# Fewer instructions for the edge lists, and earlier weights, in a four-layer graph network on one core

## The chip, the cores and the metric

The kernel runs on one core of one Trainium2 chip. A core has TensorE (PE, matrix products; PEld are its weight loads), VectorE (DVE), ScalarE (ACT), GpSimd (POOL) and SyncE (SP), each with its own queue of instructions that runs in order, and 16 DMA engines that they share. The metric is the device time of one execution, in microseconds, as the median of several runs.

## The reference

A graph of 3327 nodes with 512 features each and an integer adjacency matrix (a few edges per row, more in the first rows and columns). Four layers run on it, each as `x = layernorm(x + layer(x))`.

```python
# layer 0 and layer 3: attention over the neighbours (layer 3 builds its weights from four quaternion parts)
Wh = einsum('nd,hdo->hno', x, W)                       # 8 heads of 64
e  = leaky_relu(f1[:, :, None] + f2[:, None, :], 0.2)  # f1 = Wh.a1, f2 = Wh.a2
out = elu(softmax(where(adj > 0, e, -9e15)) @ Wh)
# layer 1: mean over the neighbours
agg = (adj > 0) @ x / max(deg, 1)
out = relu(concat(x @ W_self + b_self, agg @ W_nb + b_nb) @ W_comb + b_comb)
# layer 2: mean over the first 64 neighbours of each row, leaky relu, plus leaky relu of x @ W_line.T
```

## The kernel before

The nodes stand in 26 blocks of 128. The adjacency is sparse, so the kernel doesn't multiply with it: for each block it makes a list of its edges, and in each layer an indirect DMA (on POOL's queue, line 999) gathers the rows of the neighbours, 128 edges to a "chunk", into a ring of slots in SBUF. A product with a 0/1 selection matrix sums the gathered rows into the block's nodes (L1356 in layers 0 and 3, L1850 in layers 1 and 2). Rows are gathered in groups of up to four chunks (`GROUP`). Block 0, whose rows are dense, is done apart.

**The prologue** has three interleaved parts. `projection(b)` loads a block of x, transposes it (L783) and multiplies it with layer 0's weights (L1037), and stores the result in the table `t0_d`. `structure` reads the adjacency rows of one block after the other (L866), takes their signs on ScalarE with a running sum (L873), and makes the block's list. `fused_weights` multiplies layer 1's self and neighbour weights by its combining weights, eight tiles of 512x128, each transposed (L783 on `raw`) and multiplied (L800), and a bias product at its end (L1634). `score_weights` (L1551 to L1554) prepares layer 0's scores from the weights `w0` and the vectors `a0`. The loop over t starts a projection, then takes three steps of `structure`, and from t = 13 on one step of `fused_weights`; whatever is left of the fused weights is drained after the last projection and after `g0.head` and `g0.finish`, which complete the table.

**A list** is made so: VectorE multiplies the mask with a code of positions (L888), finds the largest eight of each of several segments (L901) and of those the largest K (L911, L913). Its degree and the entry for the first column (`dgs`, L889, L896, L897) are rounded to `dg16` (L921). TensorE turns the degrees of 128 rows into starting places with two products (L923, L924) in the PSUM tile p1; four ScalarE and three VectorE instructions (L926 to L932) take from it the biases `here`, the places `starts` and `nmids`, and the first two columns of `sl`. A further product (L935) gives the steps `dl`. Then for each span of up to ten chunks, first those that fill the room from its near end, then those of its far end, ScalarE makes a sign matrix `u` (L945), TensorE multiplies it (L952), ScalarE rounds the result (L955), and VectorE picks the edge (L960 to L973). p1, p2 and a transposed column share one PSUM bank.

The first 16 or so lists are made in the prologue, the rest during layer 0, whose `feed` takes one or two steps of `structure` for each group. Until layer 1 begins, a scheduler orders the instructions of each engine by priorities and estimates; from there (`manual_schedule`) they stand in the order of the program. The memory of the ring (22 slots of 528 floats) is lent during the prologue, in order of the calls of `lent`, to the mask of block 0, `w0`, `a0`, the rows of zeros, a scratch row, and the combining weights `wc`; a gather into a slot waits for the readers of what lay there.

`groups` takes sizes for its first groups from its argument `first`; in the kernel before only layer 3 passes `(1, 2)`.

Of the kernel before, what the change touches and what calls it, by code (L numbers as in the profile page):

```python
# [631 lines left out]
def sparse_path(ctx, tc, flag_i, x, adj, l0_w, l0_a1, l0_a2, l1_w_self, l1_b_self, l1_w_nb, l1_b_nb,  # L632
# [68 lines left out]
    starts = keep.tile([P, NL, 2], F32, name="starts")  # L701
    nmids = keep.tile([P, NL, 2], F32, name="nmids")
    for l in (l for ls in lists for l in ls):
        l.nmid = nmids[:, l.at]
# [47 lines left out]
    point5 = const.tile([P, 1], F32, name="point5")  # L752
    nc.gpsimd.memset(point5, 0.5)
# [98 lines left out]
    def structure(big, mid, ps, m0):  # L852
# [16 lines left out]
        def masks(b, ab):  # L869
            ms = []  # L870
            for s in range(2):
                m = m0[:, s * HW:(s + 1) * HW] if b == 0 else big.tile([P, HW], BF16, name="m", bufs=2)
                nc.scalar.activation(m, ab[s], AF.Sign, accum_out=half[:, s, b:b + 1])  # L873
                ms.append(m)
            return ms
# [3 lines left out]
        for k, b in enumerate(order):  # L879
# [9 lines left out]
            nc.vector.tensor_reduce(dgs[:, b - 1, 1:2], ms[0][:, :P], AX.X, ALU.add)  # L889
# [3 lines left out]
            for l in lists[b]:  # L893
                L, K, cuts, a = l.L, l.K, l.cuts, l.at
                dg = dgs[:, a, 0:1]
                nc.vector.tensor_scalar(dg, half[:, 0, b:b + 1], half[:, 1, b:b + 1], 1.0, ALU.add, ALU.max)  # L896
                nc.vector.tensor_sub(dg, dg, dgs[:, a, 1:2])  # L897
# [9 lines left out]
                sl = mid.tile([P, K + 2], F32, name="sl")  # L907
                slots = sl[:, 2:]
# [11 lines left out]
                dg16 = mid.tile([P, 2], BF16, name="dg16")  # L920
                nc.vector.tensor_copy(dg16, dgs[:, a])  # L921
                p1 = ps.tile([P, 512], F32, name="p1", tag="lp")
                nc.tensor.matmul(p1[:, 0:2], before, dg16, start=True, stop=True)  # L923
                nc.tensor.matmul(p1[:, 2:4], middle, dg16, start=True, stop=True)  # L924
                here = mid.tile([P, 2], F32, name="here")
                nc.scalar.activation(here[:, 0:1], p1[:, 0:1], AF.Identity, bias=point5, scale=-1.0)  # L926
                nc.vector.tensor_scalar(here[:, 1:2], p1[:, 1:2], -1.0, l.room - 0.5, ALU.mult, ALU.add)
                nc.scalar.copy(starts[:, a], p1[:, 0:2])
                nc.scalar.copy(sl[:, 0:1], p1[:, 0:1])
                nc.vector.scalar_tensor_tensor(sl[:, 1:2], p1[:, 1:2], 1.0 - l.room, dg, ALU.add, ALU.subtract)  # L930
                nc.scalar.activation(l.nmid[:, 0:1], p1[:, 2:3], AF.Identity, bias=ones[:, 0:1])
                nc.vector.tensor_scalar(l.nmid[:, 1:2], p1[:, 3:4], -1.0, 1.0 - 2 * l.room, ALU.mult, ALU.add)  # L932
                yield None
                p2 = ps.tile([P, 512], F32, name="p2", tag="lp")
                nc.tensor.matmul(p2[:, :K + 2], step, sl, start=True, stop=True)  # L935
# [5 lines left out]
                spans = [(0, c0, l.up) for c0 in range(0, l.up, G)] + [(1, c0, L) for c0 in range(l.down, L, G)]  # L941
                for far, c0, end in spans:
                    g = min(G, end - c0)
                    u = mid.tile([P, g * P], BF16, name="u")
                    nc.scalar.activation(u, place[:, c0 * P:(c0 + g) * P], AF.Sign, bias=here[:, far:far + 1],  # L945
                                         scale=-1.0 if far else 1.0)
                    if not far:
                        yield None
                    pv = ps.tile([P, 512], F32, name="pv")
                    for c in range(g):  # L950
# [4 lines left out]
                    nc.scalar.copy(vc[:, :g * W], pv[:, :g * W])  # L955
                    if not far:
                        yield None
                    v = vc[:, :g * W].rearrange("p (c k) -> p c k", k=W)
                    off = mid.tile([P, g, 1], I16, name="off")
                    nc.vector.tensor_sub(off[:, :, 0], (npos if far else pos)[:, c0:c0 + g], v[:, :, 1 + far])  # L960
                    eq = mid.tile([P, g, K], I16, name="eq")
                    nc.vector.tensor_tensor(eq, slot[:, None, :K].to_broadcast([P, g, K]),
                                            off.to_broadcast([P, g, K]), ALU.is_equal)
                    nc.vector.tensor_mul(eq, eq, v[:, :, 3:])
                    hit = mid.tile([P, g], I16, name="hit")
                    with nc.allow_low_precision(reason="whole numbers below 4096"):
                        nc.vector.tensor_reduce(hit, eq, AX.X, ALU.add)
                    at = l.idx[:, c0:c0 + g]
                    if far:
                        nc.vector.tensor_tensor(at, at, hit, ALU.add)  # L970
                        continue
                    nc.vector.scalar_tensor_tensor(at, hit, P + 1.0, hit, ALU.is_gt, ALU.mult)
                    nc.vector.scalar_tensor_tensor(l.dst[:, c0:c0 + g], hit, P + 1.0, v[:, :, 0],  # L973
                                                   ALU.is_gt, ALU.mult)
# [45 lines left out]
    class Gat:  # L1020
# [242 lines left out]
        def group(self, item, pools, accs, done, sall=None):  # L1263
# [22 lines left out]
            for t, k, q0, q1 in parts:  # L1286
                if q0 < q1:
                    o = t[:, q0 * P:q1 * P] if t is far else t[:, :(q1 - q0) * P]
                    nc.scalar.activation(o, place[:, (c0 + q0) * P:(c0 + q1) * P], AF.Abs,  # L1289
                                         bias=l.nmid[:, k:k + 1], scale=2.0)  # L1290
# [284 lines left out]
    code = iota("code", NP, U16, 1, 2, 0, big)  # L1575
    mid = pool_in(listlay, "l0mid")
# [3 lines left out]
    with ExitStack() as pro:  # L1580
# [10 lines left out]
        w0 = lent(DC * (D + 3 * H0)).rearrange("p (c s o) -> p c s o", c=DC, s=2)  # L1591
        for c in range(DC):
# [79 lines left out]
        for t in range(NB):  # L1672
# [3 lines left out]
            if t == 13:  # L1676
                fused.add(fused_weights())
# [509 lines left out]
```

## Time and profile before

| | |
|---|---|
| median of 3 runs | 1666.48 us (1666.45 to 1667.93) |
| profiled execution | 1770.79 us, of which the span 1769.0 |
| mean granted clock of TensorE in it | 0.928 of full |
| busy in the span | PE 86%, DVE 67%, ACT 52%, POOL 43% |
| last projection ends | 205.5 us |
| first gather of layer 0 starts | 214.5 us |
| last list's segments searched (L901) | 411 us |
| layer 0 to layer 1, first gather of layer 1 | 746 us |
| first gather of layer 2 | 1137 us |

The profiled execution is one execution with the profiler on; times of single instructions come from it. Busy times are the union of an engine's instructions; an engine's share says how full it is, not whether the end waits for it. A line number is that of the kernel before unless another is said.

### The profile page before, as it was taken

The page shows a single profiled execution, that of the slowest core. Times are in us where ns is not written, and L with a number is a line of the kernel's source. Part 1 is how long each engine was busy: PE and PEld are TensorE (multiplying, and loading weights), DVE is VectorE, ACT ScalarE, POOL GpSimd, SP SyncE. Part 2 cuts the span into 40 slices and gives each one's busy share as a digit, 9 for nine tenths or more (in the row PEclk, how much of TensorE's full clock was granted, in tenths as well). Part 3 has the DMA queues.
Part 4 walks back from the last instruction along what each step waited for, and adds up shares of the span by engine and source line. Part 5 has one row for each costly group of instructions (what it writes and reads, how often), then busy time and mean ns, then how long its engine had stood idle before and what let it go on. Part 6 is the DMA issues. An engine that isn't in the chain of part 4 may idle for free.

```text
span 1769.0 us, 24447 instructions
## 1 busy us (share of the span) xinstructions
PE 1514.6 (86%) x7266; PEld 1006.2 (57%) x7266; DVE 1187.4 (67%) x3292; ACT 911.9 (52%) x3026; POOL 753.8 (43%) x909
## 2 busy tenths in 40 slices
PE   5979848899999999889999999867799983978985
PEld 4756536656666777445555554423566763756764
DVE  8988948988567788125656785537566642857886
ACT  5879745666767778312122221201344442657897
POOL 3000146564454520164444652266666305666650
PEclk9989978999999999889999999988899996989898
DMA  8787667666665542198888995287878406677761
GB/s 257 240 279 239 212 194 239 222 198 189 190 183 159 163 132 79 66 406 296 300 292 303 336 366 201 98 284 246 268 251 267 167 37 193 183 206 211 225 204 56
DMA packets 130402, 381.99 MB, mean 216 GB/s; under 512 B 22037, under 2 KB 36477, under 8 KB 130259
## 3 DMA queue, kind: packets, MB, share of 16 engines
q0 software_dynamic: 67696, 252.97, 45.1%
q1 hardware_dynamic: 62563, 127.35, 21.4%
q8 instruction: 60, 0.98, 0.2%
q14 instruction: 83, 0.68, 0.1%
HBM read 331.89 MB, written 48.37 MB: 215 GB/s over the span
## 4 chain that ended last, share of the span: by engine, by line
PE 59%; DVE 14%; ACT 9%; issue 8%; DMA 4%; another core or an unknown queue 3%; POOL 2%; SPq 0%; ACTq 0%; POOLq 0%; DVEq 0%
PE po L800 18%; PE acc L1356 12%; PE acc L1850 9%; PE po L1037 9%; PE pt L783 3%; DVE cand L901 2%; DVE gt L1337 2%; PE acc L1244 1%; PE acc L1842 1%; DMA gm<-t_d,idx 1%; ACT h L1507 1%; DVE val L888 1%; ACT gd L1457 1%; PE acc L1929 1%
## 5 line engine op out<-in xcount | busy, mean ns | idle before, releaser
L999 POOL DMA_INDIRECT gt<-t_d,idx x201 | 201.6, 1003 | 380.0 <-DVE mx L1136 200.4
L999 POOL DMA_INDIRECT gl<-t_d,idx x265 | 263.8, 995 | 185.4 <-issue 59.4
L1356 PE MATMUL acc<-gt,sel 128*128 128x264 f32 (+3 forms) x804 | 210.7, 407 | 3.3 <-DVE gt L1337 1.3
L800 PE MATMUL po<-wn,xt 128*128 128x512 f32 x416 | 197.6, 618 | 16.8 <-ACT vc L955 5.3
L999 POOL DMA_INDIRECT gm<-t_d,idx x138 | 136.4, 988 | 133.0 <-PE acc L1850 79.5
L1356 PEld LDWEIGHTS acc<-gt,sel 128*128 128x128 f32 (+3 forms) x804 | 151.0, 197 | 41.1 <-issue 15.0
L1356 PE MATMUL acc<-gl,sel 128*128 128x260 f32 (+3 forms) x524 | 138.9, 407 | 12.1 <-issue 11.7
L800 PEld LDWEIGHTS po<-wn,xt 128*128 128x128 f32 x416 | 79.2, 197 | 103.4 <-issue 82.1
L1037 PE MATMUL po<-gt,xt 128*128 128x268 f32 x416 | 115.6, 423 | 15.4 <-ACT xt L790 11.2
L1337 DVE TENSOR_TENSOR gt<-gt,pg 128x1536 f32<-128x1536 f32 (+3 forms) x63 | 116.5, 1849 | 14.3 <-ACT sel L1332 12.8
L1356 PEld LDWEIGHTS acc<-gl,sel 128*128 128x128 f32 (+3 forms) x524 | 98.7, 198 | 31.3 <-issue 17.5
L1037 PE MATMUL po<-w,xt 128*128 128x262 f32 x416 | 101.8, 399 | 12.8 <-ACT xt L790 6.9
L1850 PE MATMUL acc<-gm,selr 128*128 128x512 f32 (+3 forms) x324 | 107.6, 455 | 5.4 <-DMA gm<-t_d,idx 5.0
L786 ACT COPY xt<-pt 128x512 f32<-128x512 f32 x81 | 47.0, 588 | 119.5 <-PE pt L783 93.7
L901 DVE MAX8 cand<-val 128x8 f32<-128x464 uint16 (+32 forms) x184 | 107.8, 619 | 0.0
L999 POOL DMA_INDIRECT gk<-t_d,idx x65 | 65.7, 1011 | 98.0 <-DMA t_d<-mean 60.3
L1037 PEld LDWEIGHTS po<-w,xt 128*128 128x128 f32 x416 | 81.0, 197 | 32.0 <-ACT xt L790 11.6
L1037 PEld LDWEIGHTS po<-gt,xt 128*128 128x128 f32 x416 | 78.4, 202 | 34.5 <-ACT xt L790 14.5
L800 PE MATMUL po<-wx,xt 128*128 128x512 f32 x208 | 93.6, 595 | 0.4 <-issue 0.3
L1289 ACT ACTIVATE far<-place,nmids 128x384 int16<-128x384 int16 (+3 forms) x167 | 87.3, 541 | 11.9 <-DVE ds L1299 9.4
L800 PE MATMUL po<-wl,xt 128*128 128x512 f32 x208 | 93.0, 592 | 0.0
L783 PE MATMUL pt<-s_ident,xres 128*128 128x128 f32 x500 | 79.1, 286 | 12.3 <-DVE xres L845 5.3
(389 smaller groups left out, 3283.0 us busy)
## 6 DMA issues: line engine op xcount, KB each, us to landing
ab<-in_adj_dram SPq DMA_DIRECT2D x25, 832.0 KB
ab<-in_adj_dram SPq DMA_DIRECT2D x25, 831.5 KB
t_d<-t SPq DMA_DIRECT2D x25, 512.0 KB
gm<-t_d POOLq DMA_DIRECT2D x23, 512.0 KB
t_d<-t SPq DMA_DIRECT2D x25, 384.0 KB
t_d<-tg SPq DMA_DIRECT2D x25, 264.0 KB
gd<-t_d SPq DMA_DIRECT2D x25, 264.0 KB
t_d<-tg SPq DMA_DIRECT2D x25, 260.0 KB
```

The costliest lines, as they stand in the source:

```text
L783: nc.tensor.transpose(pt[:, c, :], src[:, c * P:(c + 1) * P], ident)
L786: nc.scalar.copy(xt, pt)
L800: nc.tensor.matmul(po, xt[:, c, :], w[:, c], start=c == 0, stop=c == DC - 1)
L888: nc.vector.tensor_mul(val[:, s * HW:(s + 1) * HW], ms[s], code[:, s * HW:(s + 1) * HW])
L901: nc.vector.max(out=cand[:, s, :], in_=val[:, cuts[s]:cuts[s + 1]])
L999: nc.gpsimd.indirect_dma_start(out=t[:m, c, :], out_offset=None, in_=table[:, :], in_offset=bass.IndirectOffsetOnAxis(ap=l.idx[:m, c0 + c: ...
L1037: nc.tensor.matmul(pw[s], xt[:, c, :], self.w[:, c, s, :], start=c == 0, stop=c == DC - 1)
L1244: nc.tensor.matmul(self.acc[h // hh][:, h % hh, :], wt[:m, h, :], G[:m, h, :], start=False, stop=False)
L1289: nc.scalar.activation(o, place[:, (c0 + q0) * P:(c0 + q1) * P], AF.Abs, bias=l.nmid[:, k:k + 1], scale=2.0)
L1337: nc.vector.tensor_mul(Gc[:, :, :OUT], Gc[:, :, :OUT], w[:, :g].rearrange("p c (h o) -> p (c h) o", o=1).to_broadcast([P, g * H, OUT]))
L1356: nc.tensor.matmul(accs[b][s], S[:m, c, :], G[:m, c, s * hh * M:(s + 1) * hh * M], start=at + c == 0, stop=last)
L1850: nc.tensor.matmul(accs[b], chosen, parts[:, k * D:(k + 1) * D], start=at + c + k == 0, stop=k == top and at + c == n - 1)
```

## The change

Four edits. (1) The lists: the degree in the first 128 columns comes from a separate Sign with its own running sum on ScalarE, so VectorE's reduction goes; p1 is summed from five products with constants (`halves`, `rooms`) so that all eight columns come out ready, and two ScalarE copies take them; the far span joins the last near span where both fit in ten chunks. (2) The attention vectors are loaded before `w0`, and x three blocks ahead of its projection. (3) `fused_weights` starts at t = 9, and yields once more before its bias product; its `wc` is thereby lent before the rows of zeros. (4) The first two groups of layers 0, 1 and 2 have one and two chunks.

```diff
-    starts = keep.tile([P, NL, 2], F32, name="starts")
-    nmids = keep.tile([P, NL, 2], F32, name="nmids")
+    sites = keep.tile([P, NL, 4], F32, name="sites")
+    starts = sites[:, :, :2]
...
-    point5 = const.tile([P, 1], F32, name="point5")
-    nc.gpsimd.memset(point5, 0.5)
+    signs = const.tile([P, 3, 2], F32, name="signs")
+    nc.gpsimd.memset(signs, 1.0)
+    nc.gpsimd.memset(signs[:, 0], -1.0)
+    ones16 = const.tile([1, P], BF16, name="ones16")
+    nc.gpsimd.memset(ones16, 1.0)
+    halves = const.tile([1, 8], BF16, name="halves")
+    for k, v in enumerate((0.5, -0.5, 0.0, 1.0, 0.0, 0.0, 1.0, 1.0)):
+        nc.gpsimd.memset(halves[:, k:k + 1], v)
...
-                nc.scalar.activation(m, ab[s], AF.Sign, accum_out=half[:, s, b:b + 1])
+                c0 = P if b and s == 0 else 0
+                if c0:
+                    nc.scalar.activation(m[:, :P], ab[s][:, :P], AF.Sign, accum_out=dgs[:, b - 1, 1:2])
+                nc.scalar.activation(m[:, c0:], ab[s][:, c0:], AF.Sign, accum_out=half[:, s, b:b + 1])
...
-            nc.vector.tensor_reduce(dgs[:, b - 1, 1:2], ms[0][:, :P], AX.X, ALU.add)
...
-                nc.vector.tensor_scalar(dg, half[:, 0, b:b + 1], half[:, 1, b:b + 1], 1.0, ALU.add, ALU.max)
-                nc.vector.tensor_sub(dg, dg, dgs[:, a, 1:2])
+                nc.vector.tensor_add(dg, half[:, 0, b:b + 1], half[:, 1, b:b + 1])
+                nc.vector.scalar_tensor_tensor(dg, dgs[:, a, 1:2], 0.0, dg, ALU.is_equal, ALU.max)
...
-                dg16 = mid.tile([P, 2], BF16, name="dg16")
-                nc.vector.tensor_copy(dg16, dgs[:, a])
+                dg16 = mid.tile([P, 3, 2], BF16, name="dg16")
+                nc.vector.tensor_mul(dg16, signs, dgs[:, a, None, :].to_broadcast([P, 3, 2]))
                 p1 = ps.tile([P, 512], F32, name="p1", tag="lp")
-                nc.tensor.matmul(p1[:, 0:2], before, dg16, start=True, stop=True)
-                nc.tensor.matmul(p1[:, 2:4], middle, dg16, start=True, stop=True)
-                here = mid.tile([P, 2], F32, name="here")
-                nc.scalar.activation(here[:, 0:1], p1[:, 0:1], AF.Identity, bias=point5, scale=-1.0)
-                nc.vector.tensor_scalar(here[:, 1:2], p1[:, 1:2], -1.0, l.room - 0.5, ALU.mult, ALU.add)
-                nc.scalar.copy(starts[:, a], p1[:, 0:2])
-                nc.scalar.copy(sl[:, 0:1], p1[:, 0:1])
-                nc.vector.scalar_tensor_tensor(sl[:, 1:2], p1[:, 1:2], 1.0 - l.room, dg, ALU.add, ALU.subtract)
-                nc.scalar.activation(l.nmid[:, 0:1], p1[:, 2:3], AF.Identity, bias=ones[:, 0:1])
-                nc.vector.tensor_scalar(l.nmid[:, 1:2], p1[:, 3:4], -1.0, 1.0 - 2 * l.room, ALU.mult, ALU.add)
+                nc.tensor.matmul(p1[:, :8], ones16, halves, start=True, stop=False)
+                nc.tensor.matmul(p1[:, :8], ones16, rooms[:, a], start=False, stop=False)
+                d6 = dg16.rearrange("p k s -> p (k s)")
+                nc.tensor.matmul(p1[:, :6], before, d6, start=False, stop=False)
+                nc.tensor.matmul(p1[:, 3:4], ident16, d6[:, 0:1], start=False, stop=False)
+                nc.tensor.matmul(p1[:, 6:8], middle, d6[:, 1:3], start=False, stop=True)
+                nc.scalar.copy(sl[:, :4], p1[:, :4])
+                nc.scalar.copy(sites[:, a], p1[:, 4:8])
...
-                spans = [(0, c0, l.up) for c0 in range(0, l.up, G)] + [(1, c0, L) for c0 in range(l.down, L, G)]
+                spans = [[(0, c0, min(G, l.up - c0))] for c0 in range(0, l.up, G)]
+                ends = [(1, c0, min(G, L - c0)) for c0 in range(l.down, L, G)]
+                if len(ends) == 1 and spans[-1][0][2] + ends[0][2] <= G:
+                    spans[-1].append(ends.pop())
...
+    rooms = big.tile([1, NL, 8], BF16, name="rooms")
+    nc.gpsimd.memset(rooms, 0.0)
+    for l in (l for ls in lists for l in ls):
+        for k, v in ((1, l.room), (3, -l.room), (6, -2 * l.room)):
+            nc.gpsimd.memset(rooms[:, l.at, k:k + 1], float(v))
...
+        a0 = lent(2 * D).rearrange("p (s h o) -> p s h o", s=2, h=H0)
+        for s, src in enumerate((l0_a1, l0_a2)):
+            nc.sync.dma_start(a0[:, s].rearrange("p h o -> p (h o)"), row(src, H0 * OUT0))
         for c in range(DC):
...
+        for b in range(3):
+            load(xres[b], x, b)
         next(made)
...
         def projection(b):
-            load(xres[b], x, b)
+            if b + 3 < NB:
+                load(xres[b + 3], x, b + 3)
...
                     nc.scalar.copy(o[:, i, :], po)
+            yield
             pb = ps.tile([P, D], F32, name="po")
...
-            if t == 13:
+            if t == 9:
                 fused.add(fused_weights())
...
-            for item in groups(pools[0], (b,), True):
+            for item in groups(pools[0], (b,), True, () if n else (1, 2)):
...
+    nc.vector.tensor_add(deg[:, 1:], deg[:, 1:], dgs[:, :, 1])
...
-        for item in groups(ring, weave):
+        for item in groups(ring, weave, first=(1, 2)):
...
-        nexts = groups(ring, weave)
+        nexts = groups(ring, weave, first=(1, 2))
```

Within a merged span the near and the far part keep a sign, an `off` and a last instruction each; the product's rounding (L955) and L962, L964 and L967 are done once over both.

## The prediction

> **What bounds the kernel now.** I read the page's slices first, then the busy time of each engine by stage, then the timeline where a stage has a hole, and the list of groups for the price of each instruction.
>
> ```profile
> PE   5979848899999999889999999867799983978985
> DVE  8988948988567788125656785537566642857886
> ```
>
> Each digit is one fortieth of 1769 us, 44 us. TensorE is at 8 or 9 nearly all the way; the first hole is the "48" in slices 5 and 6 (220 to 265 us), where VectorE has its own hole a slice earlier. The stretches (PE, PEld, DVE, ACT, POOL busy, then clock, DMA share, GB/s) put sizes to it:
>
> ```profile
> 40.00:205.00 165.00, 148.67 (x958) 108.32 (x957) 152.71 (x645) 140.80 (x492) 0.00 (x0) 0.93 0.77 250
> 205.00:280.00 75.00, 41.94 (x220) 28.33 (x219) 46.09 (x166) 33.82 (x88) 36.42 (x38) 0.80 0.64 192
> 280.00:432.00 152.00, 133.98 (x690) 93.92 (x688) 135.55 (x441) 97.20 (x293) 86.93 (x92) 0.92 0.69 214
> 432.00:740.00 308.00, 287.42 (x1410) 198.99 (x1409) 205.56 (x473) 214.58 (x743) 106.25 (x126) 0.97 0.46 141
> ```
>
> In the prologue (40 to 205) VectorE is busy 93% and TensorE 90%: 26 projections share the chip with the edge lists of 16 blocks. From 280 to 432, while layer 0 runs and the last lists are made, both stand near 89%. After 432, where no list is left, VectorE has room (67%) and TensorE is the bound (93%). Between them, 205 to 280, no engine is busy 62% of the time. The timeline of that hole:
>
> ```profile
> 211.17 1.97 PE L783 MATMUL pt<-s_ident,raw 128*128 128x128 f32 x8
> 213.22 8.71 PE L800 MATMUL po<-gt,xt 128*128 128x512 f32 x16
> 214.52 1.55 POOL L999 DMA_INDIRECT gt<-t_d,idx  x1 [200.38 <-DVE mx L1136]
> ...
> 221.77 7.03 PE L1634 MATMUL po<-gt,bb 128*128 128x512 f32 x16
> 227.17 0.41 ACT L1275 COPY gt<-zeros 32x16 f32<-32x16 f32 x2 [4.62 <-PE po L1634]
> ...
> 240.24 0.27 ACT L955 CAST vc<-pv 128x135 int16<-128x135 f32 x1 [11.91 <-remote]
> ...
> 254.79 1.19 PE L1356 MATMUL acc<-gt,sel 128*128 128x264 f32 x2
> ```
>
> The last projection is done at 205.5. Then TensorE does only the rest of the fused layer-1 weights (two of eight tiles, then the bias product L1634) until 228.8, while gathers arrive from 214.5 on. ScalarE's first act for a layer-0 group, L1275, stands 4.6 us for L1634, because it writes a ring slot in which the combined weight still lies; everything of ScalarE behind it waits too. The first aggregation (L1356) comes at 254.8, 40 us after the first gather. Of these 40, 11.9 and a later 3.8 us are waits whose releaser the trace doesn't know.
>
> **What the Trainium skill says.** "Perfetto Trace Analysis", Identifying the Most-Contended Engine: matmul busy time is a poor measure of TensorE's load, weight-load busy is better. By that the prologue's TensorE is at 66% (108.3 of 165), so it has more room than 90% suggests. The same page, Optimizing Scalar/DVE Operations: a small VectorE operation holds the engine for about half of its profiled latency. The trace agrees: L927 starts at 195.69 and lasts 0.15 us, the next instruction starts at 195.75. "TensorE: Matmul & The Clock Gate", What's actually happening: the clock is full or half, by recent activity; the trace's 0.80 in 205 to 280 against 0.93 before it fits, so filling that hole may also lift the clock. I count nothing for it.
>
> **The change, part by part.**
>
> ```profile
> L889 DVE TENSOR_REDUCE dgs<-m 128x1 f32<-128x128 bf16 x25 | 6.9, 275 | 0.0
> L896 DVE TENSOR_SCALAR dgs<-half 128x1 f32<-128x1 f32 x25 | 5.1, 204 | 0.0
> L927 DVE TENSOR_SCALAR here<-p 128x1 f32<-128x1 f32 x25 | 3.7, 147 | 0.0
> L930 DVE SCALAR_TENSOR_TENSOR sl<-p,dgs 128x1 f32<-128x1 f32 x25 | 3.7, 149 | 0.4 <-issue 0.4
> L932 DVE TENSOR_SCALAR nmids<-p 128x1 f32<-128x1 f32 x25 | 3.7, 146 | 0.0
> ```
>
> *Lists, VectorE.* Of each of 25 lists L889, L927, L930 and L932 go, and L896 becomes a plain add like L897 (151 ns). By durations this is 275+147+149+146+53 = 770 ns; by starts (L889 holds 0.19 us, a small one 0.07) 0.46 us. In 22 of 25 lists the far end joins the last near span (blocks 3, 4, 5 don't fit in ten chunks), so L962, L964 and L967 run once, not twice: 198+274 ns become about 325 (slope of the 128x48 and 128x120 forms), the others alike, 0.43 us by durations, half of it held. Sum: 25 x 0.46 + 22 x 0.21 = 16 us held (29 by durations), about 10 in the prologue, 6 in layer 0. At 93% busy most of it is path; two thirds: **-6 in the prologue, -4 in layer 0.**
>
> *Lists, ScalarE and TensorE.* ScalarE loses L926, L928, L929, L931 (268, 167, 179, 275 ns) and a cast (about 180), and gets two copies of 170 and a split Sign (about 270 + 208 for the sum, less 120 of the long one): -0.4 us a list, off the path at 85% busy. The ping-pong at the p1 bank (L928 behind VectorE's L927, L931 behind L930: 6.7 us of waits) goes as well; I leave it inside the two thirds. TensorE gets five small products in place of two: three weight loads of 0.1 us more, +0.3 a list, +5 us in the prologue, +2.5 later. The first two need no list data and stand early in TensorE's order; the third waits for VectorE's dg16 as L923 did. Nothing new waits.
>
> *Fused weights from the ninth projection.* In the order of the built programs six of eight tiles are multiplied before the last projection now, all eight in the changed kernel. So 2.0 + 8.7 = 10.7 us of TensorE move from the hole into the prologue. With the 5 us above, 15.7 us go into 16.3 of idle by busy time, 56 by weight loads. I take a quarter as path: **+4** (0 to +12). The bias product now stands among the head's two small products, which set the first gather: **+1** (0 to +3.5). The moved loads (8 tiles of 256 KB, 2 MB of wc) ride SP's queue earlier, at a DMA share of 0.77: hidden. The big memset L1647 (3.7 us) shrinks; POOL gets some 85 tiny memsets, 3.5 us at the 0.04 us between L749 and L751, before 20 us: hidden, as POOL does nothing from 40 to 205.
>
> *x three blocks ahead, attention vectors first.*
>
> ```profile
> 11.33 0.69 DVE L1551 TENSOR_TENSOR pr<-gt 128x512 f32<-128x512 f32 x1 [6.33 <-DMA gt<-in_L_gnn_a_dram]
> ```
>
> VectorE's first real work waits for a0, behind 1 MB of w0. With a0 first it needs 0.77 MB instead of 1.57: about 5 us sooner. But three x blocks (0.77 MB, 3 us at 257 GB/s) now stand on SP ahead of the first adjacency rows, so the mask comes at 17, not 14, and the first list gains less: **-2** (0 to -4). Later x loads hide: TensorE waited 0.8 us in all for x.
>
> *First groups of 1 and 2, the hole.* ScalarE's slot no longer lies in the combined weight, TensorE's 10.7 us are gone from here, and the first group needs one gather, not four (3.75 us at 1.25 each). The score parts are ready at 216.3; a group could begin there, not at 227. Then gathers at 1.25 us pace it, but layer 0 uses one in 2.1 us (201 in 430), so they get ahead. **-12** (-5 to -17).
>
> *First groups in layers 1 and 2.* In layer 1 TensorE is on its own self products until 756.9, after which whole groups wait 9 to 11 us for rows: **-2** (0 to -4). In layer 2 only three chunks, not eight, are asked for ahead of the last own parts, but POOL's order and waits are the same there and TensorE is busy to 1150: 0 (-1 to +2). The extra groups cost half a microsecond of VectorE each, hidden in the hole and in layer 1's 57%; the new add on deg is 0.15.
>
> **Sum:** -6 -4 +4 +1 -2 -12 -2 = **-21 us** against the profiled execution, 1770.79 us (span 1769.0). The median is 1666.48, 104 less: the profiled one has a clock of 0.928 and holes without a known releaser. The terms taken lie outside those holes, so I carry -21 over: **1645**.
>
> **Rivals.** (1) *VectorE is the bound throughout*: all 29 us count, moved products cost nothing, the clock rises in the hole: -35 to -50, about 1626. For: 93% in the prologue. Against: TensorE's in-order queue beside it. (2) *Only the hole pays*: TensorE takes back what VectorE gives: -3.5 to -10, about 1660. (3) *TensorE is the bound already, so it is slower*: all 15.7 us lengthen the prologue, the bias product delays the head by 3.5, the 2.5 in layer 0 count, VectorE's relief is worth nothing, and only the hole's 12 come back: 21.7 - 12 = +10, 1676. It turns slower by over 3.3 us once the prologue grows by more than 9.3, which is a true TensorE slack in 40 to 205 below some 6 us. For: 90% busy, 12% and 26% of the prologue's chain are L800 and L1037. Against: 66% by weight loads. (4) *No change seen*: the early products hold the one p1 bank, or stop TensorE's queue, so that each list waits; 0.8 us in each of 25 lists eats the 21. For: that bank serves a list's transpose and both its products. Against: it did before, in the same order.
>
> **How the numbers follow.** A measurement of this kernel tells about 0.2%, 3.3 us, from nothing. Forecast (-10 to -35): 0.58; rival 1: 0.13; rival 2: 0.13; rival 4: 0.06; rival 3: 0.10. Faster 0.84, same 0.06, slower 0.10. Range: 1621 takes in most of rival 1, 1664 all of rival 2; beyond it on the slow side lie rivals 3 and 4 in part.
>
> **What would show it.** Right: first gather at 209 to 214 and first aggregation 12 or more sooner after it than 40; ScalarE's zeros no longer released by the bias product; VectorE's last MAX8 on val, now at 411, near 392; after that, layers 1 to 3 keep their lengths to 3 us. Wrong: the last projection later than 205, TensorE over 160 of 165 busy in the prologue, or the gain lost before layer 0 ends.

## The result and the profile after

| | before | after |
|---|---|---|
| median | 1667.62 us (1664.22 to 1671.05) | 1663.14 us (1658.64 to 1665.46) |
| ratio, 95% interval | | 0.9969 [0.996, 0.9979] |
| profiled execution | 1770.79 us (span 1769.0) | 1659.49 us (span 1657.7) |
| last projection ends | 205.5 | 213.1 |
| first gather, first aggregation of layer 0 | 214.5, 254.8 | 221.8, 232.1 |
| last MAX8 on val | 412.5 | 374.4 |
| first gather to last aggregation of layer 1 | 364.8 | 366.5 |

Faster by 4.5 us, or 0.31%, where 21 were forecast. The profiles don't stand 4.5 us but 111 us apart: the kernel before takes near 1667 us on some occasions and near 1765 on others (its only profiles are of the second kind), so a ratio is always to runs of the kernel before beside it. Up to the first aggregation the two profiles may be set side by side all the same: f1 (below), which is the kernel after near 1770 us, has its last projection, first gather and first aggregation 0.6 to 0.8 us later than the kernel after. Behind that they may not: the last MAX8, at 374.4 here, is at 402.3 in f1.

The slices of the kernel after; a slice is now 41 us:

```profile
PE   6789968999999999889999999887999996988885
DVE  7998789998567789215566677648665644779886
```

The "48" of TensorE in slices 5 and 6 has become "68". The same stretches as before (PE, PEld, DVE, ACT, POOL busy, clock, DMA share, GB/s):

```profile
40.00:205.00 165.00, 147.48 (x964) 106.35 (x964) 142.04 (x528) 133.33 (x452) 0.00 (x0) 0.93 0.73 242
205.00:280.00 75.00, 55.80 (x332) 41.49 (x331) 66.63 (x228) 45.00 (x130) 44.84 (x45) 0.84 0.79 268
280.00:432.00 152.00, 144.10 (x761) 101.94 (x760) 131.91 (x403) 111.53 (x339) 94.97 (x104) 0.97 0.76 232
432.00:740.00 308.00, 288.70 (x1354) 193.74 (x1352) 191.81 (x420) 193.19 (x669) 114.41 (x132) 0.94 0.50 161
```

From 205 to 280 TensorE is busy 55.80 us where it was 41.94, but f1, near 1770 us, has 44.64, so most of the difference isn't the change's.

In the prologue VectorE was busy 10.7 us less (152.71 to 142.04), close to the forecast's "about 10" (though by 205 it had also done 114 MAX8 on val in place of 118, 2.2 us), and yet the prologue became longer. The waits in 40 to 205 (engine and line that wait, releaser: us in total, times, longest; first one line of the kernel before, then the kernel after, by its own line numbers) say where the freed time went:

```profile
DVE val L888 <- ACT m L873: 2.6, 3, 1.4
```

```profile
DVE val L897 <- ACT m L882: 15.7, 9, 3.9
ACT vc L967 <- PE pv L964: 10.4, 7, 3.3
...
PE po L1056 <- ACT g0fall L1068: 7.8, 2, 5.0
```

VectorE stands 15.7 us for ScalarE's signs (2.6 before); ScalarE stands 10.4 us for TensorE's span products (2.3 before). The engine that was relieved now waits for those that weren't. The hole in the timeline of the kernel after:

```profile
220.80 1.13 PE L1662 MATMUL po<-gt,bb 128*128 128x512 f32 x2 [0.20 <-DVE bb L1661]
221.75 1.30 POOL L1018 DMA_INDIRECT gt<-t_d,idx  x1 [207.98 <-DVE eq L978]
...
232.05 2.07 PE L1375 MATMUL acc<-gt,sel 128*128 128x264 f32 x4
233.91 0.21 PE L934 MATMUL p<-dg,before 128*128 128x6 bf16 x1
```

The bias product (now L1662) is over at 221.9, as gathers begin, and aggregation (now L1375) follows 10.3 us after the first gather, not 40.3. ScalarE's zeros (L1294) wait nowhere for the bias product any more.

### The profile page after: what moved, and what is told of

Its sections match the earlier page's. It is cut to its first block, busy times and chain, and to the rows that moved or that the text cites. A ratio compares the mean times of both kernels' runs of the same rounds, so it can differ in the third digit from the quotient of the medians.

```text
span 1657.7 us, 24457 instructions
## 1 busy us (share of the span) xinstructions
PE 1487.2 (90%) x7305; PEld 998.9 (60%) x7341; DVE 1175.7 (71%) x3136; ACT 903.4 (54%) x3007; POOL 762.6 (46%) x994
## 4 chain that ended last, share of the span: by engine, by line
PE 63%; DVE 11%; ACT 9%; DMA 8%; issue 5%; POOL 3%; SPq 0%; ACTq 0%; DVEq 0%; POOLq 0%
PE po L806 19%; PE acc L1375 12%; PE po L1056 10%; PE acc L1879 9%; PE pt L789 3%; DMA gl<-t_d,idx 3%; DMA gt<-t_d,idx 1%; PE acc L1871 1%; PE acc L1263 1%; DVE gt L1356 1%; PE acct L1485 1%; DVE cand L909 1%; ACT m L882 1%; ACT upc L1412 1%; POOL gl L1018 1%
## 5 line engine op out<-in xcount | busy, mean ns | idle before, releaser
L1018 POOL DMA_INDIRECT gl<-t_d,idx x265 | 269.6, 1017 | 134.8 <-DMA t_d<-t 51.4
L1375 PE MATMUL acc<-gt,sel 128*128 128x264 f32 (+3 forms) x804 | 209.9, 408 | 4.4 <-DVE gt L1356 2.7
L1018 POOL DMA_INDIRECT gm<-t_d,idx x140 | 140.4, 1003 | 143.9 <-PE acc L1879 95.6
L806 PE MATMUL po<-wn,xt 128*128 128x512 f32 x416 | 193.9, 608 | 7.1 <-ACT h L1526 3.8
L1375 PEld LDWEIGHTS acc<-gt,sel 128*128 128x128 f32 (+3 forms) x804 | 153.4, 200 | 42.0 <-issue 13.9
L1375 PE MATMUL acc<-gl,sel 128*128 128x260 f32 (+3 forms) x524 | 137.5, 410 | 11.0 <-ACT r L1553 4.9
L1375 PEld LDWEIGHTS acc<-gl,sel 128*128 128x128 f32 (+3 forms) x524 | 100.4, 201 | 27.1 <-ACT r L1553 5.2
L1056 PE MATMUL po<-w,xt 128*128 128x262 f32 x416 | 97.0, 386 | 8.0 <-ACT xt L796 5.1
L1308 ACT ACTIVATE far<-place,sites 128x128 int16<-128x128 int16 (+3 forms) x167 | 87.3, 543 | 13.1 <-DVE ds L1318 12.1
L789 PE MATMUL pt<-s_ident,xres 128*128 128x128 f32 x500 | 77.5, 283 | 17.7 <-POOL gt L1668 10.5
```

Of the source, the lines that this page charges most:

```text
L789: nc.tensor.transpose(pt[:, c, :], src[:, c * P:(c + 1) * P], ident)
L806: nc.tensor.matmul(po, xt[:, c, :], w[:, c], start=c == 0, stop=c == DC - 1)
L1018: nc.gpsimd.indirect_dma_start(out=t[:m, c, :], out_offset=None, in_=table[:, :], in_offset=bass.IndirectOffsetOnAxis(ap=l.idx[:m, c0 + c: ...
L1056: nc.tensor.matmul(pw[s], xt[:, c, :], self.w[:, c, s, :], start=c == 0, stop=c == DC - 1)
L1375: nc.tensor.matmul(accs[b][s], S[:m, c, :], G[:m, c, s * hh * M:(s + 1) * hh * M], start=at + c == 0, stop=last)
```

## The experiments

In e1 to e4, f1 to f4, h1 to h4 and k1, k2 the kernel before takes 1763 to 1772 us; in g1 to g4, as in the result, it stands near 1667.5. The first ran on chips 0 (e and k), 15 (f) and 8 (h), g on chip 12, so the difference may be the chip's; nothing here tests that. A profile is of one execution, which can stand several us off its kernel's median.

### Each edit alone

e1 is edit 1 alone, e2 edit 3, e3 edit 2, e4 edit 4. Their cores, in this order:

```diff
+                nc.tensor.matmul(p1[:, :8], ones16, rooms[:, a], start=False, stop=False)
...
+            if t == 9:
+                fused.add(fused_weights())
...
+        for b in range(3):
+            load(xres[b], x, b)
...
+            for item in groups(pools[0], (b,), True, () if n else (1, 2)):
```

> Only edit 1 (the lists, with rooms, signs and sites), on the kernel before. Theory A (the prologue is bound by the round trip between ScalarE, TensorE and the adjacency loads, so VectorE's relief becomes a wait for the masks there; in layer 0 it counts): last projection within 2 us of 205.5, VectorE's waits for the signs well above 2.6 us, last MAX8 5 to 15 us sooner, time -3 to -7 us. Theory B (VectorE is the bound of both): last projection 5 us sooner, time -8 to -14. Theory C (the five products hold TensorE): time 0 to +5.

> Only edit 3 (fused weights from t = 9, one more yield), on the kernel before. Theory A (moved TensorE work lengthens the in-order prologue about as much as it empties the hole): last projection at 211 to 215, first gather 6 to 8 us later, time -2 to +5. Theory B (TensorE has room in the prologue): last projection before 208, time -8 to -12. Theory C (the hole of the profile was mostly the profiled execution's own stall, 15.7 us): first aggregation less than 30 us after the first gather even with the fused weights where they were, and this edit alone +3 to +8.

> Only edit 2 (attention vectors first, x three blocks ahead), on the kernel before. Theory A (start is worth up to 2 us, then absorbed): first score product near 6 to 7 us in place of 11.3, first sign at 15 to 17 in place of 14, time -2 to +1. Theory B (adjacency, pushed back by x, is on the path of the prologue): last projection later by 2 to 4 us, time +2 to +4.

> Only edit 4 (first groups of 1 and 2 chunks in layers 0, 1 and 2), on the kernel before. Theory A (in layer 0 the first group still waits on ScalarE for the combined weight at the ring's far end, but starts after one gather; layers 1 and 2 hide it): first aggregation 3 to 8 us sooner after the first gather, time -1 to -5. Theory B (nothing: start is set by the fused weights' end): time -1 to +1. Theory C (more groups cost more instructions on VectorE in its bound stretch): +1 to +4. Its prologue is that of the kernel before, so its profile also shows the hole a second time.

| | ratio | last projection | first gather to first aggregation |
|---|---|---|---|
| e1, lists | 1.0024 [1.0008, 1.0041] | 210.3 | 38.2 |
| e2, fused weights | 0.9988 [0.9971, 1.0005] | 210.0 | 19.4 |
| e3, x ahead | 1.0077 [1.0054, 1.0099] | 211.8 | 39.1 |
| e4, first groups | 0.9997 [0.9983, 1.0011] | 202.4 | 36.9 |

No edit pays by itself here. The lists, the fused weights and x ahead each end the last projection 4.5 to 6.2 us later. Only the fused weights close much of the hole. Against what was expected: e1 has theory A's waits for the signs (12.7 us) but theory C's time; e2's time is theory A's, with a last projection 1 us short of A's; e4's ratio is theory B's, though the aggregation comes 3.4 us sooner, as A asked; e3's 0.77% lies beyond both theories, and where it goes was not traced.

### The full change, and each edit taken out

f1 is the full change, beside three kernels that lack one edit: f2 edit 2, f3 edit 1, f4 edit 3. f2, for one, reads:

```diff
-        for b in range(3):
-            load(xres[b], x, b)
...
-            if b + 3 < NB:
-                load(xres[b + 3], x, b + 3)
+            load(xres[b], x, b)
```

> The full change, on the same chip as the kernels beside it. Alone, the parts stood at 1.0024 (lists), 0.9988 (fused weights), 1.0077 (x ahead) and 0.9997 (first groups) of the kernel before, product 1.009. Theory A (the parts need each other: each opens room that another uses): ratio 0.997 as in the first comparison, some 5 us faster. Theory B (the parts add): about 1.009, some 15 us slower where the kernel before takes 1763 us, and the 0.997 belongs to runs near 1667 us. Theory C (near 1763 us long stops of TensorE at the layers' starts cover what the change does): within 0.2% of 1. Profile, all theories: last projection near 213, last MAX8 on val 35 us sooner than without the change.

> The change without edit 2 (x is loaded by its own projection, w0 before the attention vectors). If edit 2 costs what it cost alone (1.0077), this is 0.77% or 13 us faster than the full change. If edit 2 gives the 2 us that the forecast booked, it is 0.1% slower than the full change. Profile: first mask at 14 rather than 15 us, first score product at 11 rather than 6.5, and the last projection 1 to 6 us sooner than 213 if the x loads stand in the way of the adjacency rows.

> The change without edit 1 (lists as before). Theory A, that the lists' edit is what pays in layer 0 (last MAX8 374 against 412): slower than the full change by 5 to 10 us, last MAX8 back near 400. Theory B (the lists' edit alone was 1.0024, because VectorE's relief only waits for the signs on ScalarE): faster than the full change by 0.2%, last projection 3 to 5 us sooner than 213 and VectorE's waits for the mask back to a few us.

> The change without edit 3 (fused weights from t = 13 on). Theory A, that moving the eight tiles is what makes the last projection late: last projection 4 to 5 us sooner than 213, first aggregation of layer 0 back to 35 to 40 us after the first gather, not 10, and the time slower than the full change by 5 to 12 us as the hole comes back. Theory B (the hole only moves: what the fused weights save there, they cost before): within 0.2% of the full change.

| | ratio | last projection | first gather to first aggregation | to last MAX8 |
|---|---|---|---|---|
| f1, full | 1.0013 [0.999, 1.0036] | 213.7 | 10.4 | 169.5 |
| f2, no x ahead | 0.999 [0.9974, 1.0006] | 211.4 | 10.5 | 170.9 |
| f3, no lists' edit | 0.9983 [0.9967, 0.9998] | 211.2 | 9.4 | 173.4 |
| f4, no fused weights | 1.0029 [1.001, 1.0048] | 211.4 | 35.1 | 157.5 |

The last column counts from the first aggregation. The full change, 0.3% faster in the result, shows no difference here (theory C), so the gain depends on the occasion. f3 fits theory B, but for a last projection 2.5 us sooner, not 3 to 5; f4 has theory A's hole and theory B's time; f2 is 0.2% below the full change, which fits neither figure named for it. f1 and the kernel after are the same program. At 233 they are 0.8 us apart; then the timeline of f1 has, on VectorE and TensorE:

```profile
253.75 0.36 DVE L1344 TENSOR_REDUCE sc<-pg 128x64 f32<-128x192 f32 x1 [13.13 <-remote]
256.78 0.33 PE L1328 MATMUL pg<-g0own,ds 128*128 128x48 bf16 x2 [19.22 <-DVE gt L1356]
```

where the kernel after has

```profile
242.75 0.33 PE L1328 MATMUL pg<-g0own,ds 128*128 128x48 bf16 x2 [5.22 <-DVE gt L1356]
```

Two stretches of f1, in the columns of above:

```profile
242.00:246.00 4.00, 0.00 (x0) 0.00 (x0) 0.00 (x0) 0.00 (x0) 3.09 (x4) 0.55 0.72 245
246.00:250.00 4.00, 0.00 (x0) 0.00 (x0) 0.00 (x0) 0.00 (x0) 2.83 (x4) 0.50 0.68 204
```

From 242 to 250 TensorE, VectorE and ScalarE are all idle and only POOL goes on gathering; L1344 waits for a TensorE product that, by the model of its end, was done at 236 ("remote" is a releaser that the trace doesn't know). TensorE's own gap there is 19.2 us; in the kernel after it is 5.2 at that place, with no "remote" wait in the whole profile. In the kernel before such a stop (11.9 us) lies inside the hole of 40 us. Where the hole is closed, the stop remains: f2, f3, k1 and k2 have gaps of TensorE of 15.2 to 19.1 us there too, h2 two of 10.5 and 7.8. First gather to last aggregation of layer 0 is 501.5 us before and 492.0 in f1, 456.0 in the kernel after. The 9.5 us saved in f1 pay for a first gather 7.9 us later, layer 1 takes 369.9 us in place of 364.8, and nothing is left.

Edit 2's price is seen in the waits of 40 to 80 in f1; f2 has no such line:

```profile
PE po L1056 <- ACT g0fall L1068: 7.9, 2, 5.0
```

With x early, TensorE's projection stands in line for ScalarE to empty the earlier projection's bank, 5.0 us at one go. f2's last projection is 2.3 us earlier.

### What sets the end of the prologue

The prologue of the kernel after in four parts:

```profile
40.00:80.00 40.00, 27.98 (x209) 21.24 (x209) 37.75 (x151) 29.22 (x96) 0.00 (x0) 0.86 0.81 273
80.00:120.00 40.00, 35.39 (x236) 24.25 (x236) 37.19 (x149) 30.19 (x97) 0.00 (x0) 0.84 0.71 230
120.00:160.00 40.00, 39.13 (x255) 28.54 (x254) 32.02 (x111) 36.97 (x131) 0.00 (x0) 1.00 0.82 275
160.00:200.00 40.00, 39.98 (x246) 29.09 (x244) 31.78 (x113) 31.96 (x122) 0.00 (x0) 1.00 0.62 202
```

and of the kernel before:

```profile
40.00:80.00 40.00, 36.40 (x254) 28.71 (x253) 38.34 (x161) 33.21 (x125) 0.00 (x0) 0.93 0.70 226
80.00:120.00 40.00, 33.09 (x217) 23.61 (x216) 36.24 (x156) 30.55 (x103) 0.00 (x0) 0.83 0.92 302
120.00:160.00 40.00, 36.68 (x234) 26.14 (x233) 34.53 (x145) 36.04 (x118) 0.00 (x0) 0.96 0.68 228
160.00:200.00 40.00, 38.58 (x232) 26.64 (x232) 38.91 (x161) 36.64 (x133) 0.00 (x0) 1.00 0.78 246
```

Before, TensorE had 4.7 us of idle time in 120 to 200, and 10.5 in 40 to 120. After, its second half is full (0.9 idle), VectorE is busy only 63.8 of 80 there, and TensorE's idle time stands early (16.6), where VectorE is nearly full (74.9 of 80). The moved tiles alone don't make this: e1, which has the lists' edit and no tile moved, has the same shape (16.6 idle early, 2.9 late):

```profile
40.00:80.00 40.00, 33.34 (x239) 26.62 (x238) 37.55 (x159) 31.61 (x114) 0.00 (x0) 0.87 0.64 204
80.00:120.00 40.00, 30.04 (x219) 21.85 (x217) 36.86 (x149) 30.97 (x98) 0.00 (x0) 0.84 0.84 279
120.00:160.00 40.00, 37.19 (x250) 25.92 (x249) 33.45 (x126) 35.06 (x117) 0.00 (x0) 0.94 0.81 274
160.00:200.00 40.00, 39.94 (x235) 28.48 (x234) 29.69 (x101) 32.87 (x123) 0.00 (x0) 1.00 0.64 209
```

So TensorE's work is pushed back into the second half, where it fills up. Why it starts later, these runs don't show. Two kernels test what the full half means: g1 starts the fused weights still earlier, g2 leaves out their transposes and products.

```diff
-            if t == 9:
+            if t == 4:
...
-                    rt = transposed(xp, ps, raw)
                     yield
-                    po = times(ps, rt, wc[:, s * DC:(s + 1) * DC, :])
-                    nc.scalar.copy(o[:, i, :], po)
+                    yield
+                    nc.scalar.copy(o[:, i, :], raw)
```

> The full change, but the fused weights start at t = 4 instead of 9. In the changed kernel TensorE is busy 39.1 and 40.0 of 40 us in 120 to 160 and 160 to 200, while it has 12 and 4.6 us of idle time in 40 to 80 and 80 to 120. Theory A (the second half of the prologue is bound by TensorE, so the moved tiles lengthen it): with three or so of the tiles in the early idle time, the last projection ends 5 to 10 us sooner than 213. Theory B (the early idle time is TensorE standing behind a list's product that waits for VectorE; a tile put there also waits in line, or pushes the lists back): last projection within 3 us of 213. Time against the full change: A 0.3% faster, B the same.

> The full change with the fused weights' eight tiles copied as they are loaded, not transposed and multiplied: some 8 x 4.4 = 35 us of TensorE are left out of the prologue (the loads, the ScalarE copies and the bias product stay; the output is not the reference's). Theory A (TensorE sets the end of the changed prologue): last projection 15 us or more sooner than 213, TensorE below 36 of 40 us in 160 to 200, and VectorE no longer waits for the masks. Theory B (the lists' chain through VectorE and ScalarE sets it): at most 5 us sooner.

g2 took 1649.63 us (two runs), 0.9894 [0.987, 0.9917], and its last projection ended at 195.7, 17.4 us sooner than in the kernel after. So TensorE sets the end of the changed prologue (theory A), if not alone: in the kernel after the products and transposes left out keep it busy 37.4 us (32.15 and 5.25), and 17.4 came back. With them go eight ScalarE copies of a transposed tile, 0.6 us each; at 4.9 us together they can't be the 17.4. g2's last two parts:

```profile
120.00:160.00 40.00, 34.89 (x254) 26.96 (x253) 35.94 (x133) 38.39 (x132) 0.00 (x0) 0.96 0.81 278
160.00:200.00 40.00, 35.08 (x227) 26.00 (x225) 37.56 (x139) 36.90 (x139) 0.00 (x0) 1.00 0.81 267
```

TensorE falls to 35 of 40, below theory A's 36, and VectorE and ScalarE rise to 36 to 38: the next bound is close behind. VectorE still waited 7.3 us for the masks, half of 15.7, where theory A had nothing.

g1 took 1662.95 us, 0.9969 [0.9956, 0.9982], the very ratio of the full change, with the last projection at 213.7: theory B. TensorE became full in 80 to 120 too, but its first part emptied further:

```profile
40.00:80.00 40.00, 25.51 (x182) 18.23 (x181) 38.68 (x153) 26.61 (x73) 0.00 (x0) 0.70 0.80 281
80.00:120.00 40.00, 39.79 (x276) 28.93 (x275) 35.52 (x143) 33.99 (x119) 0.00 (x0) 1.00 0.65 229
```

Starting the tiles sooner did not fill the early idle time: the order of the queues shifts with them.

### Layer 1's first groups, and the parts that pay

g3 has edit 3 and the first groups of layers 0 and 2 alone; g4 is the full change with

```diff
-        for item in groups(ring, weave, first=(1, 2)):
+        for item in groups(ring, weave):
```

> Only the fused weights from t = 9 and the first groups of layers 0 and 2: neither the lists' edit, nor x ahead, nor layer 1's first groups. If the parts' readings stand (no lists 0.9983, no x 0.999 where the full change was 1.0013), this is about 0.996 of the kernel before and faster than every kernel so far: last projection 206 to 210, first aggregation of layer 0 some 10 to 20 us after the first gather, layer 1 at 365 us. If those readings were the scatter of one order against another: 0.999 to 1.001.

> The full change without layer 1's first groups of 1 and 2. Kernels without them show 363.8 to 365.0 us from layer 1's first gather to its last aggregation, kernels with them 366.5 to 370.1. Theory A (the two small groups cost layer 1 some 2 to 5 us, where the forecast booked a gain of 2): that stretch is back at 365 or below, the whole 0.1 to 0.3% faster than the full change. Theory B (the difference is the chip, not the groups): stretch at 367 to 370 still, no difference in time.

g3: 1661.1 us, 0.9962 [0.9944, 0.998], as expected if the parts' readings stand. g4: 1660.3 us, 0.9961 [0.9947, 0.9975]. In g4 layer 1 takes 363.9 us against 366.5, theory A: the small first groups cost 2.6 us. All the profiles agree: layer 1, from first gather to last aggregation, takes 365.3 to 370.1 us in the nine with these groups and 363.4 to 365.0 in the eleven without. POOL's idle time before gathers into gm, in the kernel after and in g4 (releaser: us, times):

```profile
  PE acc L1879: 111.3, 61
```

```profile
  PE acc L1879: 96.6, 55
```

Six more times, and 14.7 us longer, POOL waits for TensorE to free a slot. That fits, but that these waits are the 2.6 us isn't shown. And g3, with neither the lists' edit nor x ahead, is as fast as g4 with both (0.9962 and 0.9961): together they are worth nothing that can be told from scatter.

### The lists' edit taken apart

> The kernel before itself, for a profile beside the others'. If the chip is the one near 1667 us: span near 1666, no wait longer than 3 us whose releaser is unknown, layers 2 and 3 near 293 and 267 us as in the changed kernel, and the stretch from first gather to first aggregation shorter than 40.3 by the 16 us of unknown waits in it: 22 to 26 us (theory A: the hole of 40 was mostly the stops). Theory B: it is still above 35. Time: 1.000.

> The full change without x ahead and without layer 1's first groups, that is, lists, fused weights, first groups of layers 0 and 2. Theory A (the lists' edit pays in layer 0, where x ahead took it back in the prologue): 0.993 to 0.995, the fastest so far. Theory B (TensorE sets the end of the prologue and layer 0 as well, so that VectorE's relief is worth nothing): 0.996, as with neither (0.9962) or both (0.9961). Last projection: A 207 to 209, B 210 to 212.

> Of the lists' edit only the split sign (no reduction on VectorE) and the merged spans; places and biases are made from two products as before. Theory A (the three more products and the changed order on TensorE are what made the lists' edit end the last projection at 210.3 and not 205.5): last projection at 203 to 206 and a ratio of 0.997 to 0.999. Theory B (the signs move work to ScalarE, and VectorE waits for them): last projection near 209 to 210, VectorE's waits for the mask above 10 us in the prologue, ratio 1.000 to 1.002.

> Only the fused weights from t = 9, on this chip. The first groups of layers 0 and 2 together with it gave 0.9962. Theory A (the hole is closed by taking the fused weights out of it; the first groups add little): 0.996 to 0.997. Theory B (both are needed: without the small first group the aggregation waits for four gathers): 0.998 to 1.000, first aggregation 15 to 20 us after the first gather rather than 9.4.

h1 is the kernel before again, h4 is e2 again. h2 is g3 with the lists' edit. h3 has of the lists' edit only the split sign and the merged spans:

```diff
-            nc.vector.tensor_reduce(dgs[:, b - 1, 1:2], ms[0][:, :P], AX.X, ALU.add)
...
+                if len(ends) == 1 and spans[-1][0][2] + ends[0][2] <= G:
+                    spans[-1].append(ends.pop())
```

| | ratio | last projection | first gather to first aggregation |
|---|---|---|---|
| h1, before | 1.0018 [0.9997, 1.0039] | 204.2 | 40.3 |
| h2 | 0.9968 [0.9954, 0.9983] | 211.9 | 10.2 |
| h3 | 0.9954 [0.9938, 0.997] | 206.4 | 35.7 |
| h4 | 0.9991 [0.9978, 1.0005] | 207.5 | 29.8 |

h1 took 1766.09 us with stops in its hole again, so its question, how long the hole is without them, stays open; it shows that 0.2% is scatter. h4 has e2's time (theory B), but the same program's first aggregation comes 29.8 us after the first gather here and 19.4 there: a gap of TensorE of 17.9 us lies in it, 6.9 the longest in e2. h2 fits theory B better: the lists' edit added to the parts that pay gains at most 0.1%. h3 stands 0.7% below e1, in another comparison, with neither theory's whole signature: the last projection is in theory A's range but for 0.4 us, VectorE waits 4.9 us for the masks, and the ratio beats both. Its profile (8.8 us over its median) has the gain in layer 0: first gather to last aggregation is 487.8 us against 497.1 in h1. So the five products seemed the culprit, and the last two kernels tried that in company: k1 undoes them in the full change,

```diff
-                nc.tensor.matmul(p1[:, :8], ones16, halves, start=True, stop=False)
-                nc.tensor.matmul(p1[:, :8], ones16, rooms[:, a], start=False, stop=False)
...
+                nc.tensor.matmul(p1[:, 0:2], before, dg16, start=True, stop=True)
+                nc.tensor.matmul(p1[:, 2:4], middle, dg16, start=True, stop=True)
```

and k2 joins h3's parts with g3's.

> The full change, but places and biases are made as before (two products, four ScalarE and three VectorE instructions on p1); the split sign, the merged spans and all else stay. Theory A (the five products and the order they bring are the step that took the forecast's gain): 0.3 to 0.7% faster than the full change's 0.9969 (or 1.0013 near 1770 us), that is 0.990 to 0.994 near 1667 us and 0.994 to 0.998 near 1765; last projection at 206 to 210, not 213, and TensorE's waits on the list product p2 for VectorE below 2 us in 40 to 202. Theory B (scatter between orders; TensorE is full in the second half of the prologue whatever the lists do): within 0.2% of the full change, last projection 212 to 214.

> The parts that paid when tried: split sign, merged spans, fused weights from t = 9, first groups of layers 0 and 2; not the five products, not x ahead, not layer 1's first groups. If the parts add (0.9954 and 0.9962): 0.992, some 13 us faster than before, the fastest. If TensorE, full in 160 to 200, takes it back: 0.995 to 0.997.

k1: 1.0016 [1.0004, 1.0027], last projection 214.2. k2: 0.9988 [0.9973, 1.0003], last projection 211.4. Theory A falls: without the five products the full change is no faster, and TensorE in 120 to 200 is nearly as full as with them:

```profile
120.00:160.00 40.00, 39.25 (x250) 28.46 (x250) 33.25 (x119) 37.32 (x135) 0.00 (x0) 1.00 0.82 272
160.00:200.00 40.00, 39.13 (x237) 28.36 (x236) 32.75 (x125) 32.73 (x125) 0.00 (x0) 1.00 0.63 201
```

Nor do the gains add: k2 should have given 0.992, and reaches neither that nor the 0.995 to 0.997 of its other theory. Why h3 by itself gains remains unexplained; with the fused weights and first groups moved as well the gain is gone.

Near 1667 us no complete version is shown to beat the changed kernel: g3 and g4 stand 2 to 3 us lower, within their intervals. Near 1765 us h2 and h3 (0.9968 and 0.9954) stand below f1 (1.0013), but they were not run beside it.

## Why the prediction was wrong, step by step

**The direction and the hole were right.** Faster was forecast, and of the signs named these came: zeros no longer released by the bias product, first aggregation 30 us sooner after the first gather (12 or more were asked for), TensorE at 147 of 165 in the prologue, not over 160. But the first gather is at 221.8, not at 209 to 214, and the last projection came after 205, which was named as a sign of being wrong.

**The step that failed is the lists' term in the prologue**, "At 93% busy most of it is path; two thirds: -6". The work removed was sized about rightly (10.7 us measured), its worth was not: VectorE was full beside two engines nearly as full, and what it lost in work it spends waiting for signs, 15.7 us in place of 2.6. Alone, the edit ended the last projection 4.8 us later. Over the whole kernel, taking it out (f3) or putting it in (h2) moves no time that can be told from scatter, so its -10 was worth about 0. Whether part of the -4 booked in layer 0 came is not shown: from first gather to last aggregation g3, without the edit, takes 463.5 us and the four kernels with it near 1667 take 451.6 to 457.6, but near 1770 f3 takes 487.8 without it and f1 492.0 with it, and g3's profiled execution stood 6.4 us over its median.

**"15.7 us go into 16.3 of idle" read a mean over 165 us.** Six of the eight tiles lie in 120 to 202 (five before), and 120 to 200 had 4.7 us of idle time. The Trainium skill, "Perfetto Trace Analysis", Optimization Strategy, says that a kernel can have regimes between which the most contended engine changes; the four parts show that here within one prologue. For TensorE's room the prediction leaned on the weight loads of the same page's Identifying the Most-Contended Engine, "66%" (the page names them together with the share of peak arithmetic, which was not worked out). Here they misled: in 160 to 200 they are busy 73% (29.09 of 40) while matmuls are at 39.98, and g2 shows that TensorE then sets the end. The measurement decides. The +4 itself was good: e2 ends the last projection 4.5 us later, h4 3.3 later than h1. The fault was to set a gain on VectorE against it.

**x ahead, -2:** the first score product came 4.8 us sooner, near the 5 forecast, and the first long sign at 15.1 (17 forecast, 14.0 before). The head start was then lost: last projection 6.2 us later in e3, 2.3 in f1 against f2. A wait of TensorE for ScalarE that was not in the sum (5.0 us at one go) goes with it; that it is the whole cost isn't shown. **Bias product in the head, +1:** last projection to first gather is 9.0 before, 8.7 after: 0. **Layer 1, -2:** +2.6 by g4. The "9 to 11 us for rows" on which it rests is no wait of TensorE in the trace of before: L1850 stands for gathers into gm 5.0 us in all, 1.0 at most (its weight loads 11.9 and 1.5). **Layer 2, 0:** not to be told apart.

**The sum again.** In place of -3 (-6 +4 +1 -2) the prologue has +7.2 (first gather 214.5 to 221.8), in place of -2 layer 1 has +1.7 (364.8 to 366.5). With -4.5 in all, about -13.5 is left for layer 0 and whatever else changed, where -16 (-12 and -4) was forecast. The prologue's 10 us, layer 1's 4 and layer 0's 2.5 make the 16.5 that were missing. That last figure is a remainder: no profile of the kernel before without the stops was had, so how much of the hole there is near 1667 us isn't known. The forecast's "the terms taken lie outside those holes, so I carry -21 over" failed near 1765 us, where a stop that had lain in the hole came into the open (f1); near 1667 us it can't be judged.

**The rivals.** Rival 2, "only the hole pays; TensorE takes back what VectorE gives", -3.5 to -10, fits what happened near 1667 us, and g2, g3 and k1 bear it out. The 1663.14 us lie in the stated range of 1621 to 1664 only because that range took this rival in, not because the forecast's own sum came out. Rival 3's premise (a true slack of TensorE below some 6 us) held for the second half, with 4.7 us; the prologue grew by 7.2, short of the 9.3 from which it would have been slower. Rival 1 is refuted by VectorE's waits. Of rival 4 nothing is seen: L931, first into the p1 bank, waits 2.3 us in the whole kernel.

## What to carry to other kernels

Before a saved microsecond on a full engine is counted, cut the stretch into parts and look at the other engines in the part where the work would move; if they are nearly full too, the saving can become a wait, as it did here. Idle time in an early part doesn't pay for work that is due in a later one. A gap that an edit closes may have been hiding another stop, so ask what else lay in it. And compare an edit with runs beside it: the same edits gave 0.9969 in one comparison and 1.0013 in another.

## What the runs showed of the hardware

One program took 1663.14 us in one comparison and 1772.47 in another (f1), with a mean granted clock of 0.955 and 0.932 in the profiled executions. Of the 111 us between their profiled spans, 36 lie in layer 0 (first gather to last aggregation 456.0 and 492.0), 24 in layer 2 (first gather to last projection 292.5 and 316.3) and 47 after it (266.2 and 313.6). There, in f1, engines wait up to 12.6 us for a releaser that the trace doesn't know, under "remote":

```profile
DVE sc L1345 <- remote: 21.0, 3, 12.6
ACT xt L796 <- remote: 15.3, 2, 9.9
```

The second line is ScalarE reading a transpose of TensorE: one that was over at 1235.6 by the model of its end is read at 1243.5. None of the five profiles near 1667 us (the kernel after, g1 to g4) has such a wait. In the stop at the start of f1's layer 0 the granted clock fell to 0.50 and stood there from 246 to 262. What stops TensorE, and whether the lower clock is more than a consequence, these runs don't show.
